# A windowed-attention and Fourier kernel on one core: the first sixteen rows transposed by TensorE, loads reordered on SyncE

## The chip, the core and the metric

The kernel runs on one core of one Trainium2 chip. Times are device microseconds of that core. The core has TensorE (PE; weight loads are shown as PEld), VectorE (DVE), ScalarE (ACT), GpSimd (POOL) and SyncE (SP), which here only issues DMAs. The metric is the device time of one execution, as the median of several.

## The reference

The input `x` is 32 images of 56 x 56 tokens with 128 channels. Two residual layers follow each other, both on a group norm of their input (`_gn`: 32 groups of four channels, over a whole image).

```
x = x + window_attention(_gn(x), rpb_table, w_qkv, w_proj, b_proj)   # windows 7x7, shifted by 3, 4 heads of 32
x = x + fourier(_gn(x), w0, w1, W1, b1, W2, b2)                      # 32 modes
```

The attention shifts the image by (-3, -3), cuts it into 8 x 8 windows of 49 tokens, forms q, k and v, adds a relative position bias and a shift mask to the scores, takes the softmax, multiplies by v and projects. The Fourier layer takes a cosine transform along the width, mixes channels for each of 32 modes, and transforms back; it does the same along the height; the sum of both goes through a feed-forward block (128 to 512, ReLU, 512 to 128).

## The kernel before

Work goes by window rows: 8 rows of 8 windows for each image, 256 in all. One *cycle* is one pass of the main loop. In cycle c row c gets q, k, v and its scores; row c-1 gets its division by the softmax sum; row c-2 gets its attention weights transposed; row c-3 gets `attn_values`, `attn_project` and its residual; row c-4 gets the sums that the second norm needs. Beside this run the Fourier layers of the one or two images before. `CONV_BEGIN` is 11: cycles 0 to 10 (`first_rows`) do attention alone; in cycles 11 to 18 image 0's transforms and mixing are added; from cycle 19 on the feed-forward groups (`FF_AT`, eight cycles after an image's Fourier work begins) are there too.

The order of instructions on TensorE, ScalarE, VectorE and GpSimd is the order in which the program writes them (`manual_schedule`). SyncE is not in that list: a scheduler sets the order of its DMAs.

These are the steps of a row that the text speaks of, with the profile's lines:

- `attn_q`, `attn_k`: TensorE products (L122), evicted by ScalarE (L444, L457). `attn_v`: L470, copied by ScalarE (L477).
- `attn_scores`: TensorE (L492); VectorE adds bias and mask while it evicts (L500, two instructions).
- `attn_max`: VectorE max (L510), then GpSimd subtracts it (L511). `attn_exp`: ScalarE (L517).
- `attn_recip`: VectorE sum `sm` (L522) and reciprocal `rs` (L524).
- `attn_divide`: GpSimd, six instructions (L536) that put the product with `rs` into `blocks`, 32-column pieces placed so that a 32 x 32 transpose inside VectorE finishes the job. `attn_transpose`: that VectorE transpose into `eT` (L546).
- `attn_values`: TensorE (L563) into two of four PSUM banks `pa`; the result `oT` is evicted half by ScalarE (L595), half by VectorE (L593).
- `attn_project`: TensorE (L608); VectorE adds the tokens `xr` (L616, "the x add"); SyncE stores the rows to `scr`.
- `attn_sums`: VectorE (L633). `attn_squares`: ScalarE squares (L645) into the `xr` buffer. `sum_squares`: VectorE (L649). `add_sums`: GpSimd (L659).
- `load_tokens` fetches `xr` (two buffers); `add_bias` on GpSimd adds the projection's bias to it (L136).

The four PSUM banks `pa` are used in turn, so the values of one row go into the bank that the projection of the row before filled, and wait for its x add.

An image comes in four quarters (`load_quarter`), which VectorE transposes (`turn_quarter`, L345 to L350) into `xw`; `row_stats` (L367) and `image_norm` (four steps) follow. Image 0's quarters lie in the buffers `y_of`, which the Fourier layer needs only later; all others use one buffer `xin`, so each quarter is loaded once the one before is turned. `rstd` of the norm is computed on GpSimd (L415), and scales the weights on ScalarE (`wn`, L423), which q, k and v use.

At the start GpSimd also clears buffers, and fetches the position bias through three steps of small DMAs (`rpb_cols`, `rpb`, and a copy of `rpb`), from which VectorE builds the mask table `bm` (L231).

Of the kernel before, what the change touches and what calls it, by code (L numbers as in the profile page):

```python
# [9 lines left out]

F32 = mybir.dt.float32
AF = mybir.ActivationFunctionType
# [4 lines left out]
S = 56  # L17
# [25 lines left out]
FF_AT = (8, 9, 10, 12, 13, 14, 15)  # L43
KB = 32
CONV_BEGIN = NWR + 3


@with_exitstack
def swin_fourier_kernel(
# [92 lines left out]

    def load_quarter(b, k, u):

        if b:
            t = work.tile([P, HW, KB], F32, tag="xin", name="xin", bufs=1)
        elif u:
            t = others[k]
        else:
            t = y_of[k][:, : S * KB].rearrange("p (w c) -> p w c", w=S)  # L150
            others.append(t[:, HW:])
            t = t[:, :HW]
        rows = slice(k * (S - KB), k * (S - KB) + KB)
# [6 lines left out]
    xins, others = {}, []  # L160
    for k in range(2):
        for u in range(2):
            xins[0, k, u] = load_quarter(0, k, u)
# [87 lines left out]
    idctw = const.tile([P, 2 * S], F32, tag="idctw", name="idctw")  # L251
    idcth = const.tile([P, S, 2], F32, tag="idcth", name="idcth")

    def back_weights(li):
        if li == 0:
            nc.gpsimd.memset(idctw, 0.0)
            nc.gpsimd.memset(idcth, 0.0)
        with nc.allow_non_contiguous_dma(reason="constant, once"):
            for blk in range(4 * li, 4 * li + 4):
                ls = slice(blk * NM // 2, (blk + 1) * NM // 2)  # L260
                modes = slice(blk // 2 * NM + blk % 2, (blk // 2 + 1) * NM, 2)
                nc.sync.dma_start(idctw[ls], idct_w[modes, li * 2 * S : (li + 1) * 2 * S])
# [7 lines left out]
    def mix_weights(k):  # L270
        dst, src = ((w1sb, w1), (w0sb, w0))[k // 4]
        m = slice(k % 4 * NM // 4, (k % 4 + 1) * NM // 4)
        nc.scalar.dma_start(dst[:, m], src[:, m])

    wff1 = const.tile([P, FF], F32, tag="wff1", name="wff1")
    b1sb = const.tile([P, NF], F32, tag="b1sb", name="b1sb")
# [20 lines left out]

    k_sb = big.tile([P, 2, NWR, WT], F32, tag="k", name="k")  # L300
    heads = const.tile([P, 2], F32, tag="heads", name="heads")
    nc.vector.memset(heads, 0.0)
# [2 lines left out]
    q_sb = big.tile([P, RT + JP - WT], F32, tag="q", name="q")  # L305
    nc.gpsimd.memset(q_sb, 0.0)
    v_sb = [big.tile([P, NP, C], F32, tag=f"v{i}", name=f"v{i}") for i in range(3)]
    a_sb = [big.tile([P, NH, NP, WT], F32, tag=f"a{i}", name=f"a{i}") for i in range(2)]

    def attn_buffer(r):  # L310
        return a_sb[r % 3 if r < CONV_BEGIN + 4 else r % 2]

    blocks = [
        big.tile([P, 2, NH * NP, KB], F32, tag=f"blocks{i}", name=f"blocks{i}") for i in range(2)
# [59 lines left out]
    def image_norm(im):  # L374
# [15 lines left out]

        nc.vector.bn_aggr(stat[:, 0:2], im.st)

        turned = small.tile([P, 32], F32, tag="turned", name="turned", bufs=2)
# [148 lines left out]

    def attn_transpose(im, i, r):

        eT = work.tile([P, NH * NP, JP], F32, tag="eT", name="eT")
        nc.vector.transpose(eT.rearrange("p t (k j) -> p k t j", k=2), blocks[r % 2])  # L546
        im.eT[i] = eT

# [381 lines left out]
    def row(r):  # L930
        return (images[r // NWR], r % NWR) if 0 <= r < NB * NWR else (None, 0)
# [47 lines left out]
    def halves_first(cycle):  # L979
        begins = [im for im, c in fourier(cycle) if c == 0]  # L980
        last, j = row(cycle - 4)
        if cycle % NWR == NWR - 1:
            norm_step(cycle)
        tokens_bias(cycle)
        im, i = row(cycle)
        behind_short = im and i == NWR - 1
        if behind_short:
            attn_q(im, i)
            attn_exp(cycle - 1)
        if cycle == CONV_BEGIN or (cycle - 1) % NWR not in EARLY:  # L990
# [10 lines left out]
        if last and cycle > CONV_BEGIN and not behind_short:  # L1001
            attn_squares(last, j)
            sum_squares(last, j)
        if not behind_short:
# [53 lines left out]
    def eighths(cycle):  # L1058
        im, i = row(cycle - 3)
        if im:  # L1060
            attn_values(im, i, cycle - 3, cycle % NWR in VALUES_BY_ACT)
            if cycle % NWR == NWR - 1:
                attn_squares(*row(cycle - 4))
        for im, c in fourier(cycle):
            if c == 0:
# [60 lines left out]
    def next_quarter(cycle):  # L1126
        b, quarter, late, _ = next_steps(cycle)
        if quarter:
            turn_quarter(images[b], *quarter)
        if late:  # L1130
            xins[(b, *late)] = load_quarter(b, *late)

    def wrap_rows(cycle):
# [41 lines left out]
    def next_begin(cycle):  # L1175
        b, quarter, _, _ = next_steps(cycle + 1)
        if quarter:
            if quarter == (0, 0):
                images[b] = image_begin(b)
            xins[(b, *quarter)] = load_quarter(b, *quarter)  # L1180
# [60 lines left out]

    ET = mybir.EngineType
    with tc.manual_schedule(engines={ET.PE, ET.Activation, ET.DVE, ET.Pool}):
        images[0] = image_begin(0)
        for k in range(2):
            for u in range(2):
                turn_quarter(images[0], k, u)
            if k:
                copy_wrap(images[0], nc.vector.tensor_copy)
            for i in range(NP * k, NP * k + NP):  # L1250
                row_stats(images[0], i)
        for _ in range(3):
            norm_step(-1)
        for r, t in ((0, 0), (0, 1), (1, 0)):
            for half in range(2):
                bias_and_mask(nc.vector, r, t, half)
        extra = big.tile([P, S, S], F32, tag="xf", name="a_extra", bufs=2)
        extra = extra.rearrange("p r w -> p (r w)")[:, : NH * NP * WT]
        extra = extra.rearrange("p (t w j) -> p t w j", t=NH, w=NP)
        a_sb.append(extra)  # L1260
        for cycle in range(NB * NWR + CONV_BEGIN + FF_AT[-1] - NWR + 1):
            if cycle < CONV_BEGIN:
                first_rows(cycle)
                continue
            halves_first(cycle)
            if not row(cycle - 3)[0]:
                eighths(cycle)
# [23 lines left out]
                columns_turn(cycle, 0)  # L1291
            columns_turn(cycle, 1)
            last_fetch(cycle)
            if cycle % NWR == NWR - 1 and row(cycle - 4)[0]:
                sum_squares(*row(cycle - 4))
                next_tokens(cycle)
            behind_max(cycle)
# [64 lines left out]
```

## Time and profile before

| what | us |
|---|---|
| three runs | 3241.44, 3242.36, 3245.40 |
| their median | 3242.36 |
| the profiled execution, its own time | 3245.96 |
| its span in the trace | 3244.2 |
| start of L500 in cycles 0, 4, 11, 19 | 29.57, 58.22, 135.68, 230.42 |

A page of the profile gives each engine's busy time and share of the span; then the span in 40 slices with the busy share in tenths, the TensorE clock that was granted (PEclk) and the DMA load; then groups of instructions with their count, busy time, mean time of one, and the idle time before them with what ended it. Windows give the same for stretches that one chooses. A wait line reads "engine, line, what it waited for: microseconds in total, times, longest". A timeline line reads "start, duration, engine, line, operation, output and inputs, count, and in brackets the idle time before and its releaser". In `128x392 f32<-128x392 f32` output and input are given as partitions x elements. Matmuls overlap in the array, so a busy time of a group is the time that it covers, not a sum.

### The profile page before, as it was taken

To read this page: it belongs to the slowest core of one execution; us is meant where nothing else is said; L and a number is where in the kernel's file an instruction comes from. 1 tells how busy PE (TensorE), PEld (TensorE's weight loads), DVE (VectorE), ACT (ScalarE), POOL (GpSimd) and SP (SyncE) were. 2 spreads that over 40 slices of the span, in tenths; PEclk is the share of its full clock that TensorE was granted. 3 is DMA by queue.
4 is the path that set the end of the run, shared out by engine and by line. 5 is a ranking of instruction groups with operands and counts; after the bars stand their busy time and mean duration, and the time that the engine had idled before them with its cause. 6 is when DMAs were issued, how large, how long until landed. Compare 5 with 4: busy or idle time off the path is not lost.

```text
span 3244.2 us, 149886 instructions
## 1 busy us (share of the span) xinstructions
PE 3133.4 (97%) x64640; PEld 2334.7 (72%) x64640; DVE 2544.5 (78%) x4791; ACT 2164.4 (67%) x3959; POOL 2339.8 (72%) x2634
## 2 busy tenths in 40 slices
PE   5589999999999999999999999999999999999999
PEld 3467777777777777777777777777777777777776
DVE  8778887878887887887888887888887878888741
ACT  3466777666677666676676676676676666776663
POOL 7777777777777777777777777777777777777741
PEclk8799999999999999999999999999999999999999
DMA  6546666656566655566656566656666656665453
GB/s 115 105 113 145 141 145 146 140 141 143 141 139 145 144 142 142 138 143 144 143 138 149 136 144 146 140 137 149 140 142 145 140 139 148 139 142 143 117 146 92
DMA packets 1171645, 448.36 MB, mean 138 GB/s; under 512 B 527690, under 2 KB 1141116, under 8 KB 1170980
## 3 DMA queue, kind: packets, MB, share of 16 engines
q1 hardware_dynamic: 1161636, 433.21, 57.0%
q8 instruction: 507, 8.31, 1.2%
q10 hardware_dynamic: 8736, 5.38, 0.6%
q14 instruction: 158, 1.29, 0.2%
q0 software_dynamic: 608, 0.17, 0.0%
HBM read 277.00 MB, written 161.48 MB: 135 GB/s over the span
## 4 chain that ended last, share of the span: by engine, by line
PE 88%; DVE 4%; ACT 3%; DMA 2%; issue 2%; SPq 1%; POOL 0%; ACTq 0%; DVEq 0%; POOLq 0%
PE pc L122 40%; PE pa L122 10%; PE pa L470 8%; PE pa L608 6%; PE pa L492 5%; PE pc L769 5%; PE pc L808 5%; PE pa L563 5%; PE pc L722 3%; DMA xin<-in_x_dram 2%; ACT z L777 1%; ACT k L457 1%; ACT xr L645 0%; PE pc L886 0%; DMA y<-in_x_dram 0%
## 5 line engine op out<-in xcount | busy, mean ns | idle before, releaser
L536 POOL TENSOR_TENSOR blocks<-a,rs 128x512 f32<-128x512 f32 x1506 | 1278.5, 856 | 414.8 <-DVE rs L524 295.7
L122 PE MATMUL pc<-xf,wff 128*64 128x512 f32 (+2 forms) x3584 | 714.5, 539 | 1.5 <-DVE xf L826 1.3
L122 PE MATMUL pc<-wff,hid 128*64 128x128 f32 x12288 | 714.1, 273 | 1.5 <-ACT hid L853 0.9
L122 PEld LDWEIGHTS pc<-wff,hid 128*64 128x64 f32 x12288 | 680.6, 137 | 10.7 <-ACT hid L853 5.7
L511 POOL TENSOR_TENSOR a<-a,mx 128x784 f32<-128x784 f32 x251 | 377.2, 1503 | 284.8 <-DVE mx L510 264.0
L122 PEld LDWEIGHTS pc<-xf,wff 128*64 128x64 f32 x3584 | 266.2, 136 | 369.7 <-issue 294.0
L853 ACT ACTIVATE hid<-pc,b1sb 128x512 f32<-128x512 f32 (+2 forms) x896 | 499.9, 642 | 41.7 <-PE pc L122 41.4
L122 PE MATMUL pa<-xw,wn 128*64 128x392 f32 x2048 | 397.6, 503 | 28.9 <-ACT wn L423 28.7
L477 ACT COPY v<-pa 128x512 f32<-128x512 f32 x256 | 151.8, 593 | 343.9 <-PE pa L470 341.1
L500 DVE TENSOR_TENSOR a<-pa,bm 128x392 f32<-128x392 f32 x502 | 259.9, 560 | 137.7 <-PE pa L492 127.9
L457 ACT ACTIVATE k<-pa,bqkv,heads 128x392 f32<-128x392 f32 x512 | 318.3, 673 | 15.1 <-PE pa L122 2.0
L546 DVE STREAM_TRANSPOSE eT<-blocks 128x1024 f32<-128x1024 f32 x256 | 314.5, 1229 | 0.9 <-POOL blocks L536 0.9
L858 POOL TENSOR_TENSOR res<-res,b2sb 128x512 f32<-128x512 f32 (+1 forms) x224 | 252.3, 1126 | 86.9 <-DMA res<-scr 71.9
L136 POOL TENSOR_TENSOR xr<-xr,bproj 128x384 f32<-128x384 f32 (+1 forms) x256 | 292.4, 1142 | 29.7 <-DMA xr<-in_x_dram 16.0
L744 ACT ACTIVATE y<-modes,rstd 128x448 f32<-128x448 f32 x256 | 276.5, 1137 | 45.2 <-DVE modes L737 31.4
L517 ACT ACTIVATE a<-a 128x784 f32<-128x784 f32 x251 | 214.8, 856 | 134.9 <-POOL a L511 134.4
L470 PE MATMUL pa<-wn,xw 128*64 128x128 f32 x4096 | 291.6, 284 | 12.1 <-issue 5.2
L444 ACT ACTIVATE q<-pa,bqkv 128x392 f32<-128x392 f32 x256 | 149.6, 584 | 230.1 <-PE pa L122 228.1
L563 PEld LDWEIGHTS pa<-eT,v 49*32 49x32 f32 x16384 | 173.6, 106 | 161.4 <-issue 68.4
L522 DVE TENSOR_REDUCE sm<-a 128x16 f32<-128x784 f32 x251 | 240.9, 960 | 56.9 <-ACT a L517 56.8
L608 PE MATMUL pa<-wproj,oT 128*64 128x128 f32 x3584 | 247.2, 277 | 21.4 <-DVE oT L593 18.9
L470 PEld LDWEIGHTS pa<-wn,xw 128*64 128x64 f32 x4096 | 227.6, 140 | 53.9 <-ACT oT L595 9.9
(113 smaller groups left out, 4891.6 us busy)
## 6 DMA issues: line engine op xcount, KB each, us to landing
zscr<-z SPq DMA_DIRECT2D x512, 112.0 KB
xin<-in_x_dram SPq DMA_DIRECT2D x496, 112.0 KB
htok<-scr SPq DMA_DIRECT2D x128, 392.0 KB
zT<-zscr SPq DMA_DIRECT2D x192, 256.0 KB
res<-scr SPq DMA_DIRECT2D x160, 256.0 KB
out_dram<-res SPq DMA_DIRECT2D x160, 256.0 KB
scr<-x SPq DMA_DIRECT2D x256, 112.0 KB
xr<-in_x_dram SPq DMA_DIRECT2D x256, 84.0 KB
```

What stands on the lines that cost most here:

```text
L122: nc.tensor.matmul(dst[ps], lhsT=lhsT[:, ps], rhs=rhs, start=start, stop=stop)
L136: nc.gpsimd.tensor_tensor(piece, piece, bproj.unsqueeze(1).to_broadcast([P, n, C]), ALU.add)
L457: nc.scalar.activation(k_sb[:, u], pk[:, :RT].rearrange("p (w j) -> p w j", j=WT), AF.Identity, bias=im.bias[:, 3 + u : 4 + u], scale=head ...
L470: nc.tensor.matmul(pv[HALVES[w % 2], w // 2 * C : (w // 2 + 1) * C], lhsT=im.half[i // NP][:, t0 : t0 + JP], rhs=im.w[:, 2 * C : 3 * C], s ...
L500: nc.vector.tensor_tensor(a[:, 2 * hp : 2 * hp + 2, :, 0:WT].rearrange("p u w j -> p w u j"), ps[hp][:, :RT].rearrange("p (w u j) -> p w u ...
L511: nc.gpsimd.tensor_tensor(a3, a3, mx.unsqueeze(2).to_broadcast([P, 2 * NWR, WT]), ALU.subtract)
L536: nc.gpsimd.tensor_tensor(dst[to, k, :, :n], a3[src, :, kb * KB : kb * KB + n], rs[src].unsqueeze(2).to_broadcast([src.stop - src.start, 2 ...
L546: nc.vector.transpose(eT.rearrange("p t (k j) -> p k t j", k=2), blocks[r % 2])
L563: nc.tensor.matmul(po4[u][h * HD : (h + 1) * HD, pr], lhsT=v[ks, pr, h * HD : (h + 1) * HD], rhs=eT[ks, h * NP + pr, :WT], start=True, sto ...
L608: nc.tensor.matmul(pp[hs, (n - n0) * C : (n - n0 + 1) * C], lhsT=oT[:, t0 : t0 + JP], rhs=wproj, start=True, stop=True,)
L744: nc.scalar.mul(y[:, r], t.rearrange("p (n k) -> p n k", k=NM), im.rstd)
L853: nc.scalar.activation(hf[:, :n], ph[:, :n], AF.Relu, bias=b1sb[:, f : f + 1])
```

## The change

The first sixteen rows (images 0 and 1, `TURNED_BY_PE`) are transposed by TensorE: `attn_divide` becomes one GpSimd instruction in place, `attn_transpose` multiplies 64-column pieces of it with an identity into two banks `pc`, and ScalarE copies the result to `eT`. The buffers `a` get a tail of 15 zero columns for that. In `first_rows` all of `oT` is evicted by ScalarE. For the first eleven rows `attn_squares` runs on GpSimd into a buffer of its own; afterwards ScalarE does it as before, but in row 6 of an image, as in row 7, it stands behind the values (`LATE_SQUARES`).

SyncE is put under the written order until cycle 10. Image 1's four quarters go into the same buffers as image 0's, and are loaded as soon as each half is turned, followed by two rows of tokens and the eight pieces of the mix weights, which ScalarE's queue issued before, one in each of cycles 2 to 9. The inverse transforms' constants are loaded in cycles 3 and 5 (before: 6 and 7), the feed-forward weights in cycle 6 (before: 8); the token loads stand at the head of a cycle.

```diff
+TURNED_BY_PE = 2 * NWR
...
     def load_quarter(b, k, u):
-        if b:
+        if b > 1:
             t = work.tile([P, HW, KB], F32, tag="xin", name="xin", bufs=1)
-        elif u:
-            t = others[k]
         else:
             t = y_of[k][:, : S * KB].rearrange("p (w c) -> p w c", w=S)
-            others.append(t[:, HW:])
-            t = t[:, :HW]
+            t = t[:, u * HW : (u + 1) * HW]
...
+    nc.gpsimd.memset(idctw, 0.0)
+    nc.gpsimd.memset(idcth, 0.0)
+
     def back_weights(li):
-        if li == 0:
-            nc.gpsimd.memset(idctw, 0.0)
-            nc.gpsimd.memset(idcth, 0.0)
...
     def mix_weights(k):
-        nc.scalar.dma_start(dst[:, m], src[:, m])
+        nc.sync.dma_start(dst[:, m], src[:, m])
...
+    ident = work.tile([P, HB], F32, tag="hid", name="ident", bufs=NF)[:, :P]
+    make_identity(nc, ident)
...
-    a_sb = [big.tile([P, NH, NP, WT], F32, tag=f"a{i}", name=f"a{i}") for i in range(2)]
+    AT = NH * NP * WT
+    a_ends = [big.tile([P, AT + JP - WT], F32, tag=f"a{i}", name=f"a{i}") for i in range(2)]
+    a_sb = [t[:, :AT].rearrange("p (t w j) -> p t w j", t=NH, w=NP) for t in a_ends]
+    for t in a_ends:
+        nc.gpsimd.memset(t[:, AT:], 0.0)
...
     def attn_divide(r, rs):
         a3 = attn_buffer(r).rearrange("p t w j -> p (t w) j")
+        if r < TURNED_BY_PE:
+            nc.gpsimd.tensor_tensor(
+                a3, a3, rs.unsqueeze(2).to_broadcast([P, 2 * NWR, WT]), ALU.mult
+            )
+            return
...
     def attn_transpose(im, i, r):
         eT = work.tile([P, NH * NP, JP], F32, tag="eT", name="eT")
+        if r < TURNED_BY_PE:
+            a2 = a_ends[r % 3]
+            for g in range(0, NH * NP, NWR):
+                pt = conv_bank()
+                for k in range(NWR):
+                    for u, hs in enumerate(HALVES):
+                        nc.tensor.matmul(
+                            pt[u * JP : (u + 1) * JP, k * WT : (k + 1) * WT],
+                            lhsT=a2[:, (g + k) * WT : (g + k) * WT + JP],
+                            rhs=ident[:, u * JP : u * JP + WT],
+                            start=True,
+                            stop=True,
+                        )
+                nc.scalar.copy(
+                    eT[:, g : g + NWR, :WT], pt[:, :RT].rearrange("p (k j) -> p k j", j=WT)
+                )
+            im.eT[i] = eT
+            return
...
-        im.sq = im.xr.pop(i)[:, : n1 - n0]
-        nc.scalar.activation(im.sq, piece, AF.Square, scale=valid)
+        if NWR * im.b + i < CONV_BEGIN:
+            im.sq = work.tile([P, HB], F32, tag="hid", name="sq", bufs=NF)
+            im.sq = im.sq.rearrange("p (n c) -> p n c", c=C)[:, : n1 - n0]
+            nc.gpsimd.tensor_tensor(im.sq, piece, piece, ALU.mult)
+        else:
+            nc.scalar.activation(im.sq, piece, AF.Square, scale=valid)
...
+    LATE_SQUARES = (6, 7)
...
     def first_rows(cycle):
+        if cycle > 3:
+            next_tokens(cycle)
...
-            attn_values(im3, i3, cycle - 3)
+            attn_values(im3, i3, cycle - 3, True)
...
-        next_tokens(cycle)
...
-        if 1 < cycle < 10:
-            mix_weights(cycle - 2)
-        if cycle in (6, 7):
-            back_weights(cycle - 6)
-        if cycle == 8:
+        if cycle in (3, 5):
+            back_weights(cycle // 2 - 1)
+        if cycle == 6:
             ff_weights()
...
+        with tc.manual_schedule(engines={ET.SP}):
+            images[0] = image_begin(0)
+            for k in range(2):
+                for u in range(2):
+                    turn_quarter(images[0], k, u)
+                if k:
+                    copy_wrap(images[0], nc.vector.tensor_copy)
+                for u in range(2):
+                    xins[1, k, u] = load_quarter(1, k, u)
+                for i in range(NP * k, NP * k + NP):
+                    row_stats(images[0], i)
+            for i in range(2):
+                load_tokens(images[0], i)
+            for m in range(8):
+                mix_weights(m)
...
+            for cycle in range(CONV_BEGIN):
                 first_rows(cycle)
-                continue
+        for cycle in range(CONV_BEGIN, NB * NWR + CONV_BEGIN + FF_AT[-1] - NWR + 1):
```

More of the change, by code (lines that the diff above doesn't have):

```diff
@@ L9 @@
 from concourse._compat import with_exitstack
+from concourse.masks import make_identity
 F32 = mybir.dt.float32
@@ L158, in load_quarter @@
         return t
-    xins, others = {}, []
+    xins = {}
     for k in range(2):
@@ L307, in swin_fourier_kernel @@
     v_sb = [big.tile([P, NP, C], F32, tag=f"v{i}", name=f"v{i}") for i in range(3)]
-    a_sb = [big.tile([P, NH, NP, WT], F32, tag=f"a{i}", name=f"a{i}") for i in range(2)]
+    AT = NH * NP * WT
[3 more added lines that the diff above has]
+        nc.gpsimd.memset(t[:, AT:], 0.0)
     def attn_buffer(r):
-        return a_sb[r % 3 if r < CONV_BEGIN + 4 else r % 2]
+        return a_sb[r % 3 if r < TURNED_BY_PE + 2 else r % 2]
     blocks = [
@@ L391, in image_norm @@
         nc.vector.bn_aggr(stat[:, 0:2], im.st)
-        turned = small.tile([P, 32], F32, tag="turned", name="turned", bufs=2)
+        turned = small.tile([P, 32], F32, tag="turned", name="turned", bufs=1)
         nc.vector.transpose(turned, stat)
@@ L1000, in halves_first @@
                 wrap_rows(cycle)
-        if last and cycle > CONV_BEGIN and not behind_short:
+        late = im and i in LATE_SQUARES
+        if last and cycle > CONV_BEGIN and not late:
             attn_squares(last, j)
             sum_squares(last, j)
-        if not behind_short:
+        if not late:
             next_tokens(cycle)
@@ L1061, in eighths @@
             attn_values(im, i, cycle - 3, cycle % NWR in VALUES_BY_ACT)
-            if cycle % NWR == NWR - 1:
+            if row(cycle)[0] and cycle % NWR in LATE_SQUARES:
                 attn_squares(*row(cycle - 4))
@@ L1129, in next_quarter @@
             turn_quarter(images[b], *quarter)
-        if late:
+        if late and (b, *late) not in xins:
             xins[(b, *late)] = load_quarter(b, *late)
@@ L1179, in next_begin @@
                 images[b] = image_begin(b)
-            xins[(b, *quarter)] = load_quarter(b, *quarter)
+            if (b, *quarter) not in xins:
+                xins[(b, *quarter)] = load_quarter(b, *quarter)
     def first_rows(cycle):
@@ L1243, in swin_fourier_kernel @@
     with tc.manual_schedule(engines={ET.PE, ET.Activation, ET.DVE, ET.Pool}):
[L1244 to L1262, printed above, removed]
+        with tc.manual_schedule(engines={ET.SP}):
[13 more added lines that the diff above has]
+                mix_weights(m)
+            for _ in range(3):
+                norm_step(-1)
+            for r, t in ((0, 0), (0, 1), (1, 0)):
+                for half in range(2):
+                    bias_and_mask(nc.vector, r, t, half)
+            extra = big.tile([P, S, S], F32, tag="xf", name="a_extra", bufs=2)
+            extra = extra.rearrange("p r w -> p (r w)")[:, : AT + JP - WT]
+            nc.gpsimd.memset(extra[:, AT:], 0.0)
+            a_ends.append(extra)
+            a_sb.append(extra[:, :AT].rearrange("p (t w j) -> p t w j", t=NH, w=NP))
+            for cycle in range(CONV_BEGIN):
                 first_rows(cycle)
-                continue
+        for cycle in range(CONV_BEGIN, NB * NWR + CONV_BEGIN + FF_AT[-1] - NWR + 1):
             halves_first(cycle)
@@ L1293, in swin_fourier_kernel @@
             last_fetch(cycle)
-            if cycle % NWR == NWR - 1 and row(cycle - 4)[0]:
+            if row(cycle)[0] and cycle % NWR in LATE_SQUARES:
                 sum_squares(*row(cycle - 4))
```

## The prediction

> **What bounds the kernel now.** I read the page's busy table and slices, then windows, then the order of single instructions. A *cycle* c is the pass in which row c (8 rows per image, 256 in all) gets its scores; its mark is the start of VectorE's bias add (L500).
>
> ```profile
> PE 3133.4 (97%) x64640; PEld 2334.7 (72%) x64640; DVE 2544.5 (78%) x4791; ACT 2164.4 (67%) x3959; POOL 2339.8 (72%) x2634
> PE   5589999999999999999999999999999999999999
> PEclk8799999999999999999999999999999999999999
> ```
>
> TensorE is full, and its clock at nine tenths or more, from the fourth slice (81 us each) on. Row to row, eight cycles there take 96.42 us at best and 97.2 in the mean: what isn't TensorE work is below 1 us per image. The change touches that part only in one order (below), so everything else is decided before cycle 19, the first with feed-forward work (L500 at 230.42). There the windows show
>
> ```profile
> 60.00:80.00 20.00, 15.36 (x280) 11.12 (x278) 19.79 (x37) 9.02 (x17) 17.90 (x21) 0.74 0.63 151
> 200.00:220.00 20.00, 13.93 (x378) 11.67 (x380) 16.90 (x33) 9.08 (x18) 13.57 (x16) 0.83 0.51 123
> 500.00:600.00 100.00, 99.92 (x2086) 74.62 (x2082) 82.16 (x156) 68.88 (x128) 76.15 (x86) 1.00 0.61 143
> ```
>
> (columns: PE, PEld, DVE, ACT, POOL busy, clock, DMA). VectorE is the fullest engine early, and TensorE waits for it (PE's waits, 30 to 130 us):
>
> ```profile
> PE pa L608 <- DVE oT L593: 18.9, 6, 7.4
> PE pa L492 <- ACT k L457: 6.1, 8, 1.4
> PE pa L563 <- DVE eT L546: 5.0, 2, 3.4
> ```
>
> Over 30 to 130 us VectorE itself waited 12.6 us for image quarters (xin), three times. One cycle without such a wait, on VectorE:
>
> ```profile
> 114.72 1.03 DVE L500 TENSOR_TENSOR a<-pa,bm 128x392 f32<-128x392 f32 x2
> 115.79 0.97 DVE L510 TENSOR_REDUCE mx<-a 128x16 f32<-128x784 f32 x1
> 116.67 0.68 DVE L649 TENSOR_REDUCE part<-xr 128x32 f32<-128x512 f32 x1
> 117.27 0.96 DVE L522 TENSOR_REDUCE sm<-a_extra 128x16 f32<-128x784 f32 x1
> 118.26 0.25 DVE L524 RECIPROCAL rs<-sm 128x16 f32<-128x16 f32 x1
> 118.43 1.19 DVE L546 STREAM_TRANSPOSE eT<-blocks 128x1024 f32<-128x1024 f32 x1
> 119.54 0.52 DVE L616 TENSOR_TENSOR x<-pa,xr 128x384 f32<-128x384 f32 x1
> ```
>
> Then come row_stats, the sum L633 and the oT eviction, and L500 again at 122.92: 8.2 us, back to back. So VectorE's own work is the cycle.
>
> **What the skill says.** "TensorE: Matmul & The Clock Gate", What's actually happening: after an idle window of about 3.4 us the array falls to half clock. The trace agrees: after the waits of 4.4 to 7.4 us the sixteen L470 matmuls take 1.9 to 2.0 us, elsewhere 1.09. Same page, Architectural detail: only TensorE pulls anything ahead, the other engines are strict FIFO; L500 to L616 above stand in program order. "SBUF — State Buffer", SBUF: two separate sides: VectorE and GpSimd share a port pair under an exclusive lock; here the tiny multiply L399 of the norm took 0.19 us at 20.52 and 1.08 at 83.54, beside GpSimd's divides.
>
> **The change, part by part.**
>
> *Start.* GpSimd's order: the identity takes the gap (18.2 to 20.2) in which the two blocks memsets (1.85) stood; they, the q memset (0.45) and small ones now follow the rpb DMA, which ended at 21.41, and stand ahead of rstd. So rstd starts at 23.9, not 21.77: wn, q, k and all of cycle 0 are **2.1 us later**. The mask adds on VectorE wait with it (nb is ahead of them) and end just in time. On SyncE image 1's sixteen DMAs start at 18.85, as two quarters' did; 0.56 us of issue each. Image 0 (1.8 MB) filled the DMA engines for 12.5 us, so image 1 lands by about 34, ahead of cycle 2's use (44). The eight mix DMAs leave ScalarE (8 × 0.33 us of issue, no wait shown: worth 0) and land by 48 to 60. Behind them on SyncE stand row 0's store, twelve idct DMAs (0.45 each, cycle 3 now, 6 before) and row 2's tokens: about 62, used at 66. Twelve more (cycle 5) and six feed-forward loads (cycle 6) stand ahead of rows 4 and 5, with 7 us or more to spare. Cost 0 if so, up to 4 if the weights are slow; nothing gained, as no wait of before names these loads.
>
> *Cycles 2 to 4.* The divide falls from six instructions (5.34) to one on 128x784, priced by the subtract of that form, 1.50: −3.8 on GpSimd. It is ahead of row 0's turn, for which TensorE waited 3.4 us, and quarter 1's xin wait (2.4) goes. L500 of cycle 3 comes 3.8 earlier, of cycle 4 5.0 earlier, before the 2.1 is taken off.
>
> *The turn.* 32 matmuls per row, nearest row L886 (64 columns, 64-column weights): 20.7 us for 512, 40 ns each, so 1.3 us per row; 2.2 at half clock. ScalarE gets two copies (128x392, 0.57 each) and oT's three more pieces (0.6), and loses the squares (0.6 to 0.7): 4.4 to 5.5 us per cycle, not the bound. VectorE loses eT (1.19) and oT (0.65).
>
> *The squares.* Here is the new wait. attn_squares goes to GpSimd, in whose order it stands behind the subtract, which waits for the max; and VectorE's sum of squares is right behind the max. Subtract 1.50, squares 1.00 or 1.27 (the add of the same shape, L136), handovers 0.3: VectorE stands still **2.9 us** with sm, rs and the x add behind it; the next row's values matmuls wait for the x add's bank. From L500: adds 1.08, max 0.97, wait 2.9, sum 0.5, sm 1.0, rs 0.2, x add 0.6: 7.25. Then either quarter (1.95), stats (1 or 1.95) and sum (0.6) on VectorE, or values and scores on TensorE (0.75 + 0.85): a cycle is 9.0 to 10.8. What left VectorE (1.84) is less than what it waits.
>
> *Marks.* Before, and after by this sum (2.1 included): cycle 4: 58.2, 55.3; 5: 66.3, 65.1; 6: 75.4, 75.9; 7 (norm, without its port conflict): 87.0, 87.6; 8: 102.9, 103.7; 9: 114.7, 113.7; 10: 122.9, 123.6. Cycle 8 keeps its wait: image 2's quarter is issued, in program order, behind row 4's store after cycle 7's x add: store 0.8, four issues 2.2, landing 3.4, turn 1.7. The change moved image 1's loads, not these. Cycles 4 to 9 thus cost 3.6 more. Cycle 10 waits for GpSimd's squares twice: 14.6 against 12.76, 1.8 more (138.2).
>
> *Cycles 11 to 18.* TensorE isn't full and rows 9 to 15 are turned there. By the chain, eT and the divide mostly lay beside other work; the matmuls stand ahead of v, and the copies ahead of v's copy, the y scales and exp. Per cycle: 11: −1.2 (divide out of rstd's way); 12: 0 (waits for xin); 13: +1; 14: +1.3 (TensorE-bound); 15: −2 (norm free of the port, rstd not behind a divide); 16: −1.5; 17 and 18: −1.2 to the mark of 19. Sum −3.6.
>
> *From 19.* The only edit is squares late in row 6 too. It takes ScalarE's wait for the x add off the z copies; TensorE's loss in that cycle sums to 1.3 us over the run. I take −1.
>
> Total: +2.1 −5.0 +3.6 +1.8 −3.6 −1 = **−2.1 us**. The profiled execution took 3245.96 (span 3244.2 and 1.8 around it), 3.6 over the median; off the median of 3242.36 that is 3240.
>
> Unknown ends: identity 0 to +2 (it may outlast the gap), transposes 1.0 to 2.2 a row (−4 to +14, hidden where VectorE is late), row 2's tokens 0 to +4, late squares −5 to +3.
>
> **Rivals.** (0.2%, 6.5 us, is about what a measurement here can tell from no change.)
>
> *A, gain in full, 3217, chance 0.25.* If VectorE's relief reached the path in cycles 4 to 10 (7 × 1.84 = 12.9) and stages 11 to 18 gave 10 (the divide's 3.8 in three cycles), with 2.9 at the start: −26. For it: VectorE's 19.79 of 20 us, and the clock, which would rise with shorter gaps. Against: the FIFO order of max, subtract, squares, sum.
>
> *B, slower, 3258, chance 0.23.* The new wait leaves TensorE idle over 3.4 us per cycle, and it stays at half clock: values and scores 2.5 instead of 1.65, in seven cycles +6, turns and transforms in 11 to 18 +1.5 a cycle, 12: about +18 on my sum. It decides from a gap of 3.4 us; my sum has 9.0 less 6.6 busy, 2.4.
>
> *C: the moved loads help nothing*, since image 2's quarters bound cycle 8 anyway. That is in my sum; if row 2's tokens also came late, 3244. It counts with my case.
>
> **Numbers.** My case (C with it) has 0.52, own range 3231 to 3250; of it 0.15 faster, 0.33 within, 0.04 slower. Adding A and B: faster 0.40, same 0.33, slower 0.27. The range 3220 to 3256 leaves out the far halves of A and B.
>
> **What would show it.** VectorE waits for GpSimd's squares about 2.5 to 3 us a cycle from 4 to 10; rstd at 24; L500 of cycle 10 near 123.6, of 19 near 229; the wait for xin in cycle 8 still 5 to 6 us; PEclk above 0.74. A mark of cycle 10 below 115 proves A, clocks of 0.7 through 160 us prove B; a period of eight rows off 97.2 by over 0.3 would break "only before 19".

## The result, and the profile after

The changed kernel took 3237.21 us (median of 17 runs, 3233.13 to 3240.71), the kernel before 3243.99 beside it (17 runs, 3238.34 to 3248.48): ratio 0.9979, 95% interval 0.9972 to 0.9987. That is 6.8 us less, where the prediction's sum was 2.1 less; 3237.21 is 2.8 below its forecast of 3240. The interval excludes no change, but 6.8 us is hardly more than the 6.5 that the prediction took for the least that can be told. The profiled execution took 3239.0 (span 3236.4).

The page's busy table and slices of the changed kernel:

```profile
PE 3148.4 (97%) x65664; PEld 2348.9 (73%) x65664; DVE 2516.3 (78%) x4751; ACT 2183.5 (67%) x4004; POOL 2294.3 (71%) x2570
PE   5789999999999999999999999999999999999999
PEclk9899999999999999999999999999999999999999
```

TensorE has 1024 records more, the turn of sixteen rows. TensorE's busy share in the second slice rose from 5 to 7 tenths, and its granted clock in the first two from 8 and 7 tenths to 9 and 8. The windows (PE, PEld, DVE, ACT, POOL busy, clock, DMA):

```profile
60.00:80.00 20.00, 15.25 (x403) 12.10 (x400) 13.89 (x24) 11.10 (x24) 11.09 (x11) 0.91 0.29 59
200.00:220.00 20.00, 18.31 (x458) 14.07 (x460) 15.78 (x32) 9.38 (x19) 16.63 (x19) 0.91 0.48 116
500.00:600.00 100.00, 99.91 (x2130) 74.98 (x2130) 81.80 (x155) 70.74 (x132) 74.76 (x85) 1.00 0.61 143
```

Before, VectorE was busy for 19.79 of the 20 us from 60 on; now no engine is full there. What VectorE does instead stands first among its waits of 30 to 130 us (total, times, longest):

```profile
DVE part L683 <- POOL sq L677: 19.2, 8, 2.7
DVE a L506 <- PE pa L498: 4.4, 4, 1.6
DVE xw L351 <- DMA xin<-in_x_dram: 3.9, 1, 3.9
```

The prediction showed VectorE back to back in the pass from mark 9 to mark 10 (8.2 us). The same pass after the change, on VectorE; the bias add is now L506, the sum of squares L683, the x add L645:

```profile
110.98 1.04 DVE L506 TENSOR_TENSOR a<-pa,bm 128x392 f32<-128x392 f32 x2 [0.34 <-PE pa L498]
112.05 0.97 DVE L516 TENSOR_REDUCE mx<-a 128x16 f32<-128x784 f32 x1
115.72 0.69 DVE L683 TENSOR_REDUCE part<-sq 128x32 f32<-128x512 f32 x1 [2.70 <-POOL sq L677]
116.33 0.96 DVE L528 TENSOR_REDUCE sm<-a_extra 128x16 f32<-128x784 f32 x1
117.32 0.25 DVE L530 RECIPROCAL rs<-sm 128x16 f32<-128x16 f32 x1
117.50 0.56 DVE L645 TENSOR_TENSOR x<-pa,xr 128x384 f32<-128x384 f32 x1
```

and on GpSimd in the same stretch:

```profile
113.19 1.50 POOL L517 TENSOR_TENSOR a<-a,mx 128x784 f32<-128x784 f32 x1 [2.99 <-DVE mx L516]
114.65 1.04 POOL L677 TENSOR_TENSOR sq<-x 128x512 f32<-128x512 f32 x1
```

Max, subtract, squares and sum of squares stand one behind the other. The transposition (1.19 us) and the oT eviction (0.66) have left VectorE, and 2.70 us of standing still has come: this pass takes 9.32 us, not 8.2.

In the table below a mark is the start of VectorE's bias add in a cycle, as in the prediction; "row 6" is the mean time from the scores of row 6 to those of row 7 of an image, by the starts of TensorE's score matmuls over rows 24 to 247. The ratio is to the kernel before, with its interval; the kernels ran on several chips, so ratios are compared and not medians.

| kernel | mark 0 | 4 | 10 | 19 | row 6 | median us | ratio |
|---|---|---|---|---|---|---|---|
| before | 29.57 | 58.22 | 122.92 | 230.42 | 10.16 | | 1 |
| after | 30.98 | 56.34 | 120.30 | 227.21 | 9.97 | 3237.21 | 0.9979 [0.9972, 0.9987] |
| e1, after without late row 6 | 31.59 | 57.55 | 121.52 | 228.18 | 10.14 | 3239.57 | 0.9993 [0.9984, 1.0001] |
| e2, before + late row 6 | 29.08 | 56.42 | 119.89 | 227.13 | 9.97 | 3235.83 | 0.9985 [0.9979, 0.9992] |
| e8, before + loads | 29.59 | 56.81 | 119.61 | 225.73 | 10.14 | 3242.62 | 0.9991 [0.9985, 0.9998] |
| e10, before + turn | 30.19 | 55.21 | 114.33 | 221.34 | 10.16 | 3229.37 | 0.9964 [0.9950, 0.9977] |
| e5, after, squares first | 31.23 | 55.87 | 108.02 | 214.92 | 9.97 | 3221.23 | 0.9939 [0.9926, 0.9953] |
| e3, after, squares on ScalarE | 31.49 | 56.15 | 109.07 | 214.96 | 9.97 | 3223.38 | 0.9928 [0.9915, 0.9942] |
| e6, after, blocks later | 29.84 | 54.75 | 119.22 | 225.05 | 9.97 | 3235.24 | 0.9965 [0.9952, 0.9977] |
| e4, after without the turn | 31.50 | 57.62 | 133.84 | 254.62 | 9.97 | 3256.18 | 1.0049 [1.0036, 1.0062] |
| e9, e5 without the turn | 31.29 | 57.13 | 122.05 | 239.55 | 9.97 | 3248.13 | 1.0006 [0.9998, 1.0015] |
| e7, three edits | 29.76 | 54.60 | 105.08 | 208.20 | 9.97 | 3217.29 | 0.9912 [0.9899, 0.9926] |

Each row's marks are of one execution. Two rows show how far those wander: e2 changes nothing ahead of cycle 11 and its mark 10 is 3.0 us off, e1 nothing either and its mark 10 is 1.2 off. Differences of marks under about 3 us are therefore not taken for an effect, unless a row of the trace names it.

### The profile page after: what moved, and what is told of

It reads as the page before. It is cut to its first block, busy times and chain, and to the rows that moved or that the text cites. A ratio compares the mean times of both kernels' runs of the same rounds, so it can differ in the third digit from the quotient of the medians.

```text
span 3236.4 us, 151985 instructions
## 1 busy us (share of the span) xinstructions
PE 3148.4 (97%) x65664; PEld 2348.9 (73%) x65664; DVE 2516.3 (78%) x4751; ACT 2183.5 (67%) x4004; POOL 2294.3 (71%) x2570
## 4 chain that ended last, share of the span: by engine, by line
PE 50%; DMA 0%; issue 0%; ACT 0%; DVE 0%; SPq 0%; DVEq 0%; ACTq 0%
PE pc L124 23%; PE pa L124 5%; PE pa L476 4%; PE pc L803 4%; PE pa L498 3%; PE pa L637 3%; PE pa L592 3%; PE pc L842 3%; PE pc L756 2%; PE pc L920 0%; DMA zT<-zscr 0%; ACT hid L887 0%; PE pa L703 0%; DMA out_dram<-res 0%; ACT xf L865 0%
## 5 line engine op out<-in xcount | busy, mean ns | idle before, releaser
L547 POOL TENSOR_TENSOR blocks<-a,rs 32x272 f32<-32x272 f32 (+3 forms) x1434 | 1217.4, 856 | 389.2 <-DVE rs L530 271.6
L506 DVE TENSOR_TENSOR a<-pa,bm 128x392 f32<-128x392 f32 x500 | 259.0, 560 | 166.0 <-PE pa L498 153.7
L575 DVE STREAM_TRANSPOSE eT<-blocks 128x1024 f32<-128x1024 f32 x240 | 295.3, 1230 | 0.0
L476 PE MATMUL pa<-wn,xw 128*64 128x128 f32 x4096 | 281.5, 279 | 1.6 <-issue 1.2
L516 DVE TENSOR_REDUCE mx<-a 128x16 f32<-128x784 f32 x250 | 242.2, 969 | 7.6
L476 PEld LDWEIGHTS pa<-wn,xw 128*64 128x64 f32 x4096 | 219.7, 137 | 36.5 <-issue 2.4
```

What stands on the lines that cost most here:

```text
L476: nc.tensor.matmul(pv[HALVES[w % 2], w // 2 * C : (w // 2 + 1) * C], lhsT=im.half[i // NP][:, t0 : t0 + JP], rhs=im.w[:, 2 * C : 3 * C], s ...
L506: nc.vector.tensor_tensor(a[:, 2 * hp : 2 * hp + 2, :, 0:WT].rearrange("p u w j -> p w u j"), ps[hp][:, :RT].rearrange("p (w u j) -> p w u ...
L547: nc.gpsimd.tensor_tensor(dst[to, k, :, :n], a3[src, :, kb * KB : kb * KB + n], rs[src].unsqueeze(2).to_broadcast([src.stop - src.start, 2 ...
```

## The experiments

**Theory** of the whole: up to cycle 19 the change is nearly a wash, because GpSimd's order (subtract, then squares) hands VectorE a wait in place of the work that it lost; most of the 6.8 us comes after cycle 19, from the one order changed there. **Rivals**: all of the gain is made by cycle 19; the wait for the squares lies beside something else; what is won by cycle 10 is lost again by cycle 19.

**The squares of row 6 (e1, e2).** e1 takes that order out of the changed kernel, e2 puts it alone into the kernel before. Row 6 stands for the cycle in which row 6 gets its scores; the squares in it are those of the row four before. Their sum and the next load of tokens move with them.

```diff
-    LATE_SQUARES = (6, 7)
+    LATE_SQUARES = (7,)
```

```diff
+    LATE_SQUARES = (6, 7)
...
-            if cycle % NWR == NWR - 1:
+            if row(cycle)[0] and cycle % NWR in LATE_SQUARES:
                 attn_squares(*row(cycle - 4))
```

> The changed kernel with LATE_SQUARES = (7,): in row 6 of an image the squares stand ahead of the values again; the start, the loads and the turned rows stay. Theory (most of the gain is made after cycle 19, by the squares in row 6): the marks of cycles 0 to 19 stay within 0.5 us of the changed kernel's (19 at 227.2), the cycle of row 6 goes from 9.97 back to 10.16 us, an image from 97.00 to 97.20, and the run takes about 5 us more than the changed kernel, 2 below the kernel before. Rival (the fill gives the gain, and the 0.2 us per image are between two executions): the rows' period stays at 97.0, and the run stays near 3237.

> The kernel before with one part of the change alone: the squares stand behind the values in rows 6 and 7 of an image, not in row 7 alone. Theory (that order is worth 5 us over the 28 images of the steady part): marks of cycles 0 to 10 as in the kernel before (10 at 122.9), the cycle of row 6 at 9.97 instead of 10.16, total 5 us below the kernel before, about 3239. Rival (the fill gives the gain): no difference from the kernel before.

Measured: e1 0.9993, e2 0.9985. Alone the order is worth 0.15% or 4.9 us (0.0008 to 0.0021, 2.6 to 6.8); without it the change is at 0.07%, 2.3 us, and its interval takes in no difference at all; the prediction's sum for everything ahead of cycle 19 was 1.1. Row 6 goes to 10.14 in e1 and to 9.97 in e2, as the theory said; the rival falls. The difference of 0.16 to 0.19 us comes in each image, 5 us over the 28 counted, and it is the same in all kernels of the table: 9.97 with the late squares, 10.14 to 10.16 without. TensorE's timeline of the same row 6 shows where, first before, then after (L470 and L476 are the v product, behind the scores):

```profile
1236.20 0.89 PE L492 MATMUL pa<-k,q 64*49 64x98 f32 x32
1237.16 1.09 PE L470 MATMUL pa<-wn,xw 128*64 128x128 f32 x16
```

```profile
1230.12 0.89 PE L498 MATMUL pa<-k,q 64*49 64x98 f32 x32
1230.95 1.09 PE L476 MATMUL pa<-wn,xw 128*64 128x128 f32 x16
```

0.96 us from the scores to v before, 0.83 after. In this cycle ScalarE evicts all of oT in both kernels, not half of it, and the v product takes the bank that this eviction frees. ScalarE before, then after:

```profile
1235.19 0.62 ACT L645 ACTIVATE xr<-x,valid 128x384 f32<-128x384 f32 x1
1235.71 1.06 ACT L777 COPY z<-pc 128x512 f32<-128x512 f32 x2
1236.65 1.06 ACT L595 ACTIVATE oT<-pa,bqkv 128x196 f32<-128x196 f32 x4
```

```profile
1229.12 1.08 ACT L811 COPY z<-pc 128x512 f32<-128x512 f32 x2
1230.22 1.04 ACT L624 ACTIVATE oT<-pa,bqkv 128x196 f32<-128x196 f32 x4
1231.13 0.63 ACT L679 ACTIVATE xr<-x,valid 128x384 f32<-128x384 f32 x1
```

With the squares behind it the eviction starts 0.10 us after the scores begin, not 0.45. Counting the holes between TensorE's records, the kernel before has one in front of v in row 6 of each of the 28 images (3.3 us together), e1 too (2.7), the changed kernel and e2 none. They are about 0.1 us in an image, so they account for more than half of the difference in row 6; where the rest of it lies was not found.

**The order of squares and subtract (e5), and the engine (e3).** Both are the changed kernel but for a place in `first_rows` (e5) or the engine in `attn_squares` (e3).

```diff
+        if last:
+            attn_squares(last, j)
         if im:
             attn_scores(im, i, cycle)
             attn_max(cycle)
         if last:
-            attn_squares(last, j)
             sum_squares(last, j)
```

```diff
-            nc.gpsimd.tensor_tensor(im.sq, piece, piece, ALU.mult)
+            nc.scalar.activation(im.sq, piece, AF.Square, scale=valid)
```

> The changed kernel with attn_squares written ahead of attn_scores and attn_max in first_rows, so that GpSimd squares the row before it subtracts the max, and VectorE's sum of squares no longer waits behind max and subtract. Theory (this wait of 2.5 to 2.7 us in each cycle took what VectorE was relieved of, and VectorE is still the cycle): the wait falls to below 0.5 us, a cycle from 5 to 10 is shorter by 1 to 2.5 us except cycle 8, which waits for image 2's quarter; the mark of cycle 10 comes 5 to 10 us earlier than 120.3, the mark of 19 by 4 to 9 (227.2 to about 220), the total by as much, 3229 to 3233. Rival 1 (the wait is beside TensorE's row of values, projection and scores, which is the cycle): the wait goes, the marks move by less than 2 us, total 3236 to 3238. Rival 2 (what is won by cycle 10 is lost in 11 to 18, where image 0's transforms wait for GpSimd or for image 2's loads): the mark of 10 is 5 or more earlier, that of 19 by less than 2.

> The changed kernel with the squares of the first eleven rows on ScalarE again, at the same place in the written order and into the same buffer of their own; everything else stays. Theory (the harm was done by GpSimd's order, subtract ahead of squares, not by moving the squares as such): on ScalarE they stand ahead of exp and behind k's eviction and wait for nothing late, so VectorE's wait for them is below 1 us, the mark of cycle 10 is at 107 to 112 as with the squares written first on GpSimd (108.0), total 3220 to 3226. Rival (ScalarE, with the turn's two copies and all of oT, becomes the cycle): exp comes later, VectorE waits for exp ahead of sm, the mark of cycle 10 is at 113 to 119, total 3226 to 3236.

Measured: e5 0.9939, e3 0.9928; against the 0.9979 of the change that is 13 and 17 us, with overlapping intervals, so engine and order are not told apart, and need not be: either one takes the wait away. Nothing here speaks for having moved the squares to GpSimd at all. In e5 VectorE's waits of 30 to 130 us have 2.5 us for the squares (three times), not 19.2. Mark 10 is 12.3 us earlier than after the change, mark 19 12.3 too: nothing is lost on the way, and both rivals of e5 fall. The theory had asked for only 5 to 10 by mark 10. The rival of e3 falls with mark 10 at 109.07: from 60 to 80 us ScalarE was busy for 16.11 of 20 and did not hold up the cycle. One pass of e5 on VectorE, from mark 5 to mark 6:

```profile
63.21 1.04 DVE L506 TENSOR_TENSOR a_extra<-pa,bm 128x392 f32<-128x392 f32 x2 [0.83 <-PE pa L498]
64.28 0.97 DVE L516 TENSOR_REDUCE mx<-a_extra 128x16 f32<-128x784 f32 x1
65.90 0.69 DVE L683 TENSOR_REDUCE part<-sq 128x32 f32<-128x512 f32 x1 [0.65 <-POOL sq L677]
66.50 0.96 DVE L528 TENSOR_REDUCE sm<-a 128x16 f32<-128x784 f32 x1
...
71.43 1.03 DVE L506 TENSOR_TENSOR a<-pa,bm 128x392 f32<-128x392 f32 x2
```

In this pass, which took 10.25 us after the change with the same wait of 2.70, VectorE now waits for 0.65 and takes 8.2 us with a quarter's turn and statistics in it (the lines left out); its own work is nearly all of the cycle again. From 60 to 80 us it is busy for 17.98 us and the granted clock is 1.00:

```profile
60.00:80.00 20.00, 17.22 (x538) 13.68 (x536) 17.98 (x40) 14.00 (x33) 12.26 (x12) 1.00 0.39 74
```

**The turn (e4, e9, e10).** e4 and e9 take TensorE's turn out, of the changed kernel and of e5; e10 puts it alone into the kernel before, with oT on ScalarE, while squares, loads and SyncE's order stay. e4, and e9 on top of e5:

```diff
-TURNED_BY_PE = 2 * NWR
+TURNED_BY_PE = 0
...
-        return a_sb[r % 3 if r < TURNED_BY_PE + 2 else r % 2]
+        return a_sb[r % 3 if r < CONV_BEGIN + 4 else r % 2]
```

e10, in the kernel before, with the changed kernel's `ident`, `a_ends`, `attn_divide` and `attn_transpose` (and, as there, one buffer instead of two for `turned`, a small tile of the norm):

```diff
+TURNED_BY_PE = 2 * NWR
...
-            attn_values(im3, i3, cycle - 3)
+            attn_values(im3, i3, cycle - 3, True)
```

> The changed kernel with TURNED_BY_PE = 0: divide in six GpSimd instructions and transpose on VectorE in all rows, as before the change; the loads, the squares on GpSimd and the oT evictions by ScalarE stay. Theory (the turn by TensorE takes 1.2 us off VectorE in a cycle that VectorE sets, and 3.8 off GpSimd ahead of row 0's turn): the mark of cycle 4 comes 3 to 5 us later than 56.3, that of cycle 10 by 8 to 12 (to 128 to 132), that of 19 by 6 to 12; total 3243 to 3249, so that the change without its TensorE part would be a loss. Rival (VectorE's transpose would lie in its wait for the squares, and GpSimd's long divide beside it): the marks of cycles 5 to 10 move by less than 3 us together, total 3237 to 3240.

> The changed kernel with the squares ahead of the subtract and with TURNED_BY_PE = 0: divide in six GpSimd instructions and transpose on VectorE in all rows. With the squares behind the subtract, taking the turn from TensorE had cost 19 us. Theory 1 (the turn is worth what it takes off the two engines: VectorE 1.2 us a cycle in seven cycles, GpSimd's divide 3.8 ahead of row 0's turn and in two or three cycles of 11 to 18): mark of cycle 10 at 118 to 122 instead of 108.0, that of 19 at 230 to 237 instead of 214.9, total 3237 to 3243. Theory 2 (most of those 19 us came from the squares standing in GpSimd's queue behind divides of 5.3 us, so they go together with the order): mark of 10 at 111 to 115, that of 19 at 220 to 225, total 3226 to 3231.

> The kernel before with one part of the change alone: the turn of the first sixteen rows by TensorE, with the one-piece divide in place and all of oT evicted by ScalarE; squares on ScalarE, loads and SyncE's order as before. Theory (the parts add, and the turn is the one that pays: the changed kernel with squares on ScalarE reached cycle 19 15.5 us ahead of the kernel before, of which the loads alone gave 4.7): mark of cycle 10 at 109 to 114 instead of 122.9, that of 19 at 218 to 221 instead of 230.4, total 9 to 13 us below the kernel before, so lower than the whole change. Rival (the turn pays only with the loads, because image 1's quarters set the first cycles otherwise): mark of 19 at 224 or later, total within 6 us of the kernel before.

Measured: e4 1.0049, e9 1.0006, e10 0.9964. Without the turn the change loses 16 us against the kernel before; e4's expectation was too small: its mark 10 is 13.5 us later than after the change (8 to 12 said), mark 19 is 27 (6 to 12 said), though mark 4 only 1.3 (3 to 5 said). Its rival falls. Theory 2 for e9 falls: with the squares first the turn is worth as much (0.67%, 22 us) as with the squares behind (0.70%, 23). Its mark 10 of 122.05 is theory 1's; mark 19 is 2.5 beyond that theory's end. GpSimd's timeline of e9 shows why, in a pass of 9.4 us from divide to divide:

```profile
74.19 5.34 POOL L547 TENSOR_TENSOR blocks<-a,rs 128x512 f32<-128x512 f32 x6 [0.29 <-ACT k L463]
79.62 1.26 POOL L138 TENSOR_TENSOR xr<-xr,bproj 128x512 f32<-128x512 f32 x1
80.84 0.83 POOL L677 TENSOR_TENSOR sq<-x 128x384 f32<-128x384 f32 x1
81.63 1.50 POOL L517 TENSOR_TENSOR a<-a,mx 128x784 f32<-128x784 f32 x1
83.09 0.32 POOL L693 TENSOR_TENSOR tot<-tot,part 128x64 f32<-128x64 f32 x1
```

The sum is 9.25 us: with six-piece divides and the squares GpSimd is the cycle in this pass, and from 60 to 80 us it is busy for 18.47 us (12.26 in e5). The one-piece divide takes 1.50. By these durations what the turn takes off GpSimd, 3.8 us a row, is its larger part as long as the squares are there, and the 1.2 off VectorE the smaller; no run takes one without the other. e10, the turn alone, is 11.7 us below the kernel before (7.5 to 16.2), its ratio lower than that of the whole change (0.9964 against 0.9979), with intervals that overlap; the rival, at 6 us or less, falls. Mark 10 at 114.33 and mark 19 at 221.34 are 0.3 above what the theory gave. There the passes from mark 5 to 7 take 8.27 and 8.24 us (8.22 and 8.38 in e5); for xin VectorE waits longer, 17.6 us between 30 and 130 us.

**Loads and start (e8, e6).** e8 is the kernel before with image 1's quarters in the buffers of image 0, loaded as in the changed kernel:

```diff
-        if b:
+        if b > 1:
...
+            for u in range(2):
+                xins[1, k, u] = load_quarter(1, k, u)
             for i in range(NP * k, NP * k + NP):
```

e6 is the changed kernel with the memsets of `blocks` behind rstd:

```diff
-    for t in blocks:
-        nc.gpsimd.memset(t, 0.0)
...
         for _ in range(3):
             norm_step(-1)
+            for t in blocks:
+                nc.gpsimd.memset(t, 0.0)
```

> The kernel before with one part of the change alone: image 1's four quarters go into the buffers of image 0 and are loaded as soon as each half is turned; the mix weights stay on ScalarE's queue, squares, turn and divide as before, SyncE's order left to the scheduler. Theory (a wait for xin of 2.4 us in cycle 2 goes, the rest of VectorE's cycle stays; image 2's quarters wait for the store as ever): mark of cycle 3 at 47.5 to 48.5 instead of 50.2, that of 10 at 119 to 121 instead of 122.9, total 1 to 3 us below the kernel before, which is inside what can be told. Rival (the two other waits for xin of before, 12.6 us in three, go too): mark of cycle 10 at 111 to 114, total 8 to 11 lower.

> The changed kernel with the two memsets of blocks (1.86 us on GpSimd) behind the first norm's rstd instead of ahead of it. Theory (they delay rstd, and all of cycle 0 with it): rstd at 22.0 instead of 23.9, marks of cycles 0 to 10 earlier by 1.5 to 2, that of 19 by 1 to 2, total 3235 to 3236. Rival (image 1's quarters or the mix weights, which don't move, set a cycle before 8): the mark of cycle 0 is 1.9 earlier, that of cycle 8 less than 0.7.

Measured: e8 0.9991, 2.9 us (0.6 to 4.9), as expected, with mark 10 in its range and mark 3, at 49.20, 0.7 beyond it. Two of the three waits for xin go, not one, but the one left is longer (7.89 us instead of 6.71, one cycle later), so the rival falls all the same. e6: rstd starts at 22.01 instead of 23.88, marks 4, 8, 10 and 19 are 1.6, 1.1, 1.1 and 2.2 earlier, for 8 and 10 a little less than the theory asked and more than the rival. The trace names the 1.9 us at the start; whether they reach the end the ratio of 0.9965 does not settle, its interval overlaps that of the change.

**Three edits (e7).** e5 and e6 together, and in `first_rows` the loads of image 2's quarters ahead of the row's store:

```diff
         turn(cycle)
+        next_begin(cycle)
         if im3:
             attn_project(im3, i3)
...
-        next_begin(cycle)
```

> Three edits to the changed kernel together: squares ahead of the subtract in first_rows, the memsets of blocks behind the first norm, and the loads of image 2's quarters issued ahead of the row's store instead of behind it. Theory (three waits in series on VectorE's path): 18 us from the first as measured, 1.5 to 2 from the second, 2 to 4 in cycle 8 from the third (its wait for xin was 4.9 with the first edit alone): mark of cycle 10 at 102 to 105, total 3215 to 3219. Rival (in cycle 11 to 13, image 0's transforms and ScalarE's queue, where cycle 12 took 16.4 us with the first edit, set the end): mark of 10 as said, that of 19 at 213 to 215, total 3219 to 3222.

Measured: 0.9912 (0.9899 to 0.9926), 28.5 us below the kernel before (24 to 33), and its interval lies below that of the change; mark 10 is at 105.08, where 102 to 105 was expected. Against e5 alone it is not told apart, as the two intervals meet at 0.9926, and what each of the two added edits brings is not shown. The wait for xin in cycle 8 is 2.91 us instead of e5's 4.86. The rival falls: mark 19 is at 208.20, not at 213 or later. But of the 6.7 us by which that precedes e5's, 3.3 come in cycles 10 and 11, where e5 has a standstill of TensorE that is told of at the end.

## Why the prediction was right, and where it was not

**The sign and the main mechanism** held. VectorE waits 2.5 to 2.7 us for GpSimd's squares in each full cycle (2.9 said), and this wait, not another limit, is what swallowed the relief: moving one instruction gives it back (13 us). It fits what the Trainium skill says in "TensorE: Matmul & The Clock Gate", Architectural detail: engines other than TensorE take their instructions in order, so that squares behind a waiting subtract wait too; e5 shows it at 12.3 us by mark 10.

**The size** held less well than 3237.21 against 3240 looks. As a difference, 6.8 us stand against 2.1. The number itself is nearer mostly because the kernel before came out at 3243.99, 1.6 above the median that the sum was taken from, and that was luck. Two terms were off by about 4 us each, both too slow: cycles 4 to 9 and the part after 19. The others were too fast, by 0.6 to 1.0 each.

**Start**: +2.1 said; rstd at 23.9 was 23.88, mark 1 is 2.15 later, mark 0 1.4. The identity, bounded at 0 to 2, costs 0.29 us in GpSimd's gap.

**Cycles 2 to 4**: mark 4 said at 55.3, measured 56.34. **Cycles 4 to 9**: +3.6 said, mark 4 to mark 10 takes 63.96 us against 64.70 before, so −0.7, no difference within what marks wander. The passes to marks 5, 6 and 10 are indeed longer, by 0.9, 1.2 and 1.1 us, but 1.7 was said for each: squares take 0.83 and 1.04 us rather than 1.00 and 1.27, and the wait shrinks with them. The passes to marks 7, 8 and 9, with the norm and the waits for xin, are 4.0 shorter together (1.5 said); in the one to mark 8 xin was waited for 3.9 us and not 5 to 6. **Cycle 10**: 15.21 against 12.76, +2.45 (+1.8 said). **Cycles 11 to 18**: −3.0 from mark 11 to mark 19 (−3.6 said). Mark 19 thus came at 227.21 instead of 229.3, 2.1 off, within what marks wander.

**After 19**: this is the step that failed. I took −1 us, from TensorE's waits of 1.3 in all; e2 measured 4.9, which only the −5 to +3 among the unknown ends takes in. The hole is 0.12 us in the mean of the images: 0.07 to 0.08 in 22 of them, 0.16 to 0.33 in six. The list shows only those six: between 300 and 3000 us its line for this cause before the change is

```profile
PE pa L470 <- ACT oT L595: 1.6, 6, 0.3
```

The reason given was half right: in the lines above the z copies do start earlier, 1.00 us ahead of the scores instead of 0.49, but what TensorE waited for is the oT eviction behind them, and what stood in its way is the 0.62 us of the squares themselves. "Off 97.2 by over 0.3" was not reached (97.00 in the mean), so "only before 19" would have stood by a test that was too coarse: 0.2 us an image is most of the result.

**The turn's price**: 32 matmuls at 40 ns were said, 1.3 us a row and 2.2 at half clock. The trace has 64 records for them, two per product, and 2.07 us a row at full clock, 2.4 to 3.3 in rows 4 to 7. A record's time was multiplied by the program's count. No harm showed at the marks: TensorE is busy for 15.25 of the 20 us from 60 on, with the turns in it.

**Rivals.** B's mechanism was there in part: TensorE idles up to 4.7 us for the x add (2.4 said) and the clock is 0.74 from 80 to 100 us; but it is 0.91 from 60 to 80 and 0.83 from 100 to 120, where the kernel before had 0.74, 0.74 and 0.67 in these three windows, and the time did not grow as B had it. The line that B was judged by, a gap of 3.4 us after the idle window that the prediction cites, is not what these traces show, and the measurement decides. Between the start and cycle 19 the granted clock of the changed kernel falls to half ten times, and the longest gap between TensorE's records next to the fall is 1.7 to 3.0 us in eight of them. Ahead of the fall at 72.5 us, for one, stands a gap of 2.73; then the clock is 0.50 (behind the busy times in the window's line), and the scores take 1.56 us instead of 0.89:

```profile
72.58 1.02 PE L592 MATMUL pa<-eT,v 49*32 49x49 f32 x64 [2.73 <-DVE x L645]
73.53 1.56 PE L498 MATMUL pa<-k,q 64*49 64x98 f32 x32
72.50:75.80 3.30, 3.22 (x111) 2.88 (x112) 3.27 (x6) 1.04 (x4) 2.33 (x2) 0.50 0.23 59
```

In each of the ten TensorE was busy for less than half of the 3.4 us before. The kernel before had it too: its sixteen L470 at 67.85 took 1.95 us, not the 1.09 of "elsewhere", with no gap over 1.54 us shortly before. B was thus nearer than its 2.4 against 3.4 made it seem.

A's number (−26) is in reach: e7 takes 28.5, with the late squares in it. The relief was real, and the order withheld it. C held in part: image 2's quarter is waited for whatever happens to image 1's (3.9 us after the change, 7.9 in e8), but the moved loads alone bring 2.9 us (0.6 to 4.9), not nothing.

**The account in ratios**: each alone in the kernel before, the turn gives −11.7, the late squares −4.9, the loads −2.9, together −19.5; the whole is −6.8. The 12.7 between them are near what the order of the squares costs by e5 (13). That is a check of the size and no proof, since the parts do not simply add: taken out of the changed kernel the turn is worth 23 us, not 11.7, as six-piece divides there meet GpSimd's squares, and the later start and SyncE's written order are in none of the three.

## What to carry to other kernels

Work that is moved to another engine should go ahead of what that engine has to wait for, not behind it: here the place of one instruction was worth more than the rest of the change brought. A change of many parts is a sum with signs; run the strongest part alone before the whole. And a hole of a tenth of a microsecond in each round of a steady loop is found by comparing the time of each position in the round between two kernels; a list of the largest waits showed six of the 28.

## What had not been expected of the hardware

- One fp32 product of 49 columns with 64-column weights makes two records of TensorE (64 for 32 in the program; the v product has 16 for 8), and a row of 32 takes 2.07 us at full clock.
- The granted clock fell to half after gaps of 1.7 to 3.0 us between TensorE's records, where it had been busy for 20 to 49% of the 3.4 us before.
- A small VectorE multiply, 32 elements in each partition, takes 1.08 us in e9 and 0.19 in e5; in e9 a divide of GpSimd runs beside it, in e5 nothing. In the next norm of e5 it takes 1.19 us, beside a subtract of GpSimd. The prediction used this for cycle 7 from the Trainium skill's page "SBUF — State Buffer", SBUF: two separate sides, which tells of a port pair that one of the two engines holds at a time; here the same instruction shows it with and without the neighbour.
- In e5 TensorE stood still for 2.99 us from 119.5 on, amid the 64 turn records of one row, with no releaser but "issue"; the pass that begins there takes 16.4 us (11.7 after the change). Its cause stays open.
